# First layer of a four-layer network: order of its recurrent half against its slot routing, and the arithmetic of its slot update

## The chip, the cores and the metric

The kernel is one launch on one core of a Trainium2 chip. The metric is the device time of that launch in microseconds (us). All data is float32. Four batch elements of 1024 tokens with 128 features each go through four layers one after the other; every layer has an "attention" half and a "feed-forward" half, each followed by a residual sum and a layer norm.

## The reference, cut to what matters

Only the first layer is touched by the change. Its attention half is two stacked minGRU layers; its feed-forward half routes every token to 8 of 64 slots, updates the slots by a GRU step, lets the slots attend to one another, and reads them back.

```python
# attention half, twice in sequence (x, then its own result)
z  = sigmoid(x @ Wz.T + bz);  g = max(x @ Wh.T + bh + 0.5, sigmoid(x @ Wh.T + bh))
h_t = (1 - z_t) * h_{t-1} + z_t * g_t           # h_0 = 0.5, over the 1024 tokens
x = layernorm(x + h)

# feed-forward half
h = gelu(concat(x, mean(slots)) @ w1 + b1);  logits = (h @ w2 + b2) / (|tau| + 0.1)
alpha = softmax over the 8 largest logits of a token, 0 for the other slots
si = (alpha^T @ x) / (sum_t alpha + 1e-8)                       # 64 slots x 128
r = sigmoid(si @ Wih_r.T + bih_r + S @ Whh_r.T + bhh_r);  z likewise
n = tanh(si @ Wih_n.T + bih_n + r * (S @ Whh_n.T + bhh_n))
S_new = (1 - z) * n + z * S
q, k, v = S_new @ wq + bq, S_new @ wk + bk, S_new @ wv + bv
y = S_new + softmax(q @ k^T / sqrt(32)) @ v
y = (y - mean) * rsqrt(var + 1e-5) * ln_g + ln_b
slot_values = y @ wvp + bvp
out = (alpha @ slot_values) @ wo + bo
x = layernorm(x + out)
```

(The reference writes the minGRU in logarithms; the recurrence above is the same function.) `S` is the same initial slot table for every batch element.

## The kernel before, in words

The first layer is written as Python generators, one for each batch element or pair of elements. `weave` takes a list of generators and advances each of them to its next `yield` in turn; that gives the program its order. The engines do not run in just that order: a planner reorders the written program, by priority (earlier written first) and by when it believes inputs and buffers to be ready. In the trace, the first slot-update matmul (`pg<-slots`) runs at 78.66 us, ahead of the first routing matmul at 82.70 us, though it is written after it. Once planned, every engine works through its own queue in order.

- `l0_gru(b)` is the attention half of one batch element. It transposes the tokens to features, then does four steps (two layers by two halves of 512 tokens). A step is a matmul `ph` and a sigmoid (line 209), a VectorE combination into `gru_g` (line 211), a matmul `pz` and two sigmoids (217, 219), a GpSimd product (221) and a VectorE scan (223) that writes a half of a tile `gru_h`. Then the result is transposed back, added to `x` (234) and normalised by `norm_parts` (lines 151 to 164), which ends with a transposed copy into `xT` (136). All four batch elements are woven, each with two PSUM banks of its own.
- `l0_slots` prepares what does not depend on the tokens.
- `l0_route(b)` is the routing of one element: gelu (283), logits, the top 8 (293, 294), exp (301), the transposed weights `alT` (315), and the slot input, which ends in `siT` (332), one tile for each pair of elements.
- `l0_update(i)` is the slot update of one pair; it needs `siT` of the pair and ends in `svo` (449).
- `l0_read(b)` needs `svo` and `alT`; it finishes the first layer for one element. `l1_measure(b)` and `l1_choose` begin the second layer.

The stages are: all four `l0_gru`; then `route(0), route(1)`; then `update(0), route(2), route(3)`; then `update(1)` with `read` and `measure` of 0 and 1; then `choose(0)` with `read` and `measure` of 2 and 3. The eight PSUM banks are divided anew at two places: four pools of two during the GRU, and then `u=2, p0=3, p1=3`, where `u` is for the update and `p0`, `p1` are for two batch elements each. A new pool's bank can be written once the last user of that bank in the old pool is done.

Of the kernel before, what the change touches and what calls it, by code (L numbers as in the profile page):

```python
# [10 lines left out]
F32 = mybir.dt.float32  # L11
I32 = mybir.dt.int32
U32 = mybir.dt.uint32
AF = mybir.ActivationFunctionType
ALU = mybir.AluOpType
AX = mybir.AxisListType

B, T, D = 4, 1024, 128
P = 128
# [39 lines left out]
class Net:  # L59
# [124 lines left out]
    def l0_load(self, pool):  # L184
        def ld(name, *shape):
            return self.load(name, list(shape), pool)

        return dict(
            w1=ld("w_slot1", P, 2, DH),
            w2=ld("w_slot2", DH + 1, NS),  # L190
            wg=ld("w_gru", P, 2, 3 * D),
            wa=ld("w_slota", P, 2 * DQ + 3 * D),
            rows=ld("slot_rows", NS, 3, D),
        )

    def l0_gru(self, b, ps, w, nb, wp):

        nc = self.nc
        self.to_features(self.xN[b], b, 0, NC, ps)
        yield  # L200
        src = self.xT[b]
        for ly in range(2):
            hv = wp.tile([P, T], F32, name="gru_h", bufs=8)
            for h in range(2):
                s = slice(h * 512, h * 512 + 512)
                ph = ps([P, 512], "ph")
                self.mm(ph, w[:, 2 * ly + 1, :], src[:, s])
                g = wp.tile([P, 512], F32, name="gru_g")
                nc.scalar.activation(g, ph, AF.Sigmoid, bias=self.col(f"bh{ly}"))

                nc.vector.scalar_tensor_tensor(
                    g, ph, nb[:, 2 + ly : 3 + ly], g, ALU.add, ALU.max
                )
                pz = ps([P, 512], "pz")
                self.mm(pz, w[:, 2 * ly, :], src[:, s])
                z = wp.tile([P, 512], F32, name="gru_z")
                nc.scalar.activation(z, pz, AF.Sigmoid, bias=self.col(f"bz{ly}"))
                a = wp.tile([P, 512], F32, name="gru_a")
                nc.scalar.activation(a, pz, AF.Sigmoid, bias=nb[:, ly : ly + 1], scale=-1.0)
                yield  # L220
                nc.gpsimd.tensor_mul(z, z, g)
                yield
                nc.vector.tensor_tensor_scan(
                    hv[:, s], a, z, hv[:, 511:512] if h else 0.5, ALU.mult, ALU.add
                )
                yield
            src = hv
        r = wp.tile([P, T], F32, name="gru_h", bufs=8).rearrange("p (c d) -> p c d", d=D)
        for h in range(2):
            c1 = 4 * h  # L230
            pt = ps([P, 4, P], "pt")
            for c in range(4):
                self.tr(pt[:, c, :], src[:, (c1 + c) * P : (c1 + c + 1) * P])
            nc.vector.tensor_add(r[:, c1 : c1 + 4, :], pt, self.xN[b][:, c1 : c1 + 4, :])
            yield
            yield from self.norm_parts(wp, r[:, c1 : c1 + 4, :], b, c1, 4, ps=ps, act=True)
            yield


    def l0_slots(self, W, sp):  # L240
# [9 lines left out]
        pb = self.psb("g0", [DH, 1], "pb")  # L250
# [9 lines left out]
        brz = sp.tile([P, 3], F32, name="brz")  # L260
        for i in range(3):
            nc.vector.tensor_add(
                brz[:, i : i + 1], self.col("bih", i=i), self.col("bhh", i=i)
            )
        W.update(s2=s2, hb=hb, rt=rt, brz=brz)
# [4 lines left out]
        W["svo"] = [sp.tile([NS + 1, 2, D], F32, name=f"svo{i}") for i in range(2)]  # L270
        for i in range(2):
            nc.sync.dma_start(out=W["svo"][i][NS : NS + 1], in_=self.io["s_bo2"])
# [62 lines left out]
    def l0_update(self, i, ps, W, wp):  # L335
# [3 lines left out]
        wg, wa, rows, brz = W["wg"], W["wa"], W["rows"], W["brz"]  # L339
        wq, wk = wa[:, 0:DQ], wa[:, DQ : 2 * DQ]  # L340
        wv, wvp, wo = (wa[:, 2 * DQ + j * D : 2 * DQ + (j + 1) * D] for j in range(3))
# [3 lines left out]
        for j in range(2):  # L345
            pg = ps([P, BS], "pg")
            w = slice(j * D, (j + 1) * D)
            self.mm(pg, wg[:, 1, w], s2, start=True, stop=False)
            self.mm(pg, wg[:, 0, w], si, start=False, stop=True)

            g = wp.tile([P, BS], F32, name=f"gate{j}")
            nc.vector.tensor_scalar(g, pg, brz[:, j : j + 1], 0.5, ALU.add, ALU.mult)
            nc.scalar.activation(g, g, AF.Tanh)
            nc.vector.tensor_scalar(g, g, 0.5, 0.5, ALU.mult, ALU.add)
            rz.append(g)
        yield
        pn = ps([P, 2, BS], "pn")
        self.mm(pn[:, 1], wg[:, 1, 2 * D :], s2)
        self.mm(pn[:, 0], wg[:, 0, 2 * D :], si)
        nn = wp.tile([P, BS], F32, name="nn")  # L360
        nc.vector.scalar_tensor_tensor(
            nn, pn[:, 1], self.col("bhh", i=2), rz[0], ALU.add, ALU.mult
        )
        nc.vector.tensor_add(nn, nn, pn[:, 0])
# [5 lines left out]
        nc.vector.tensor_mul(snf, snf, rz[1])  # L370
        nc.vector.tensor_add(snf, snf, nn)
# [3 lines left out]
        for w, nm in ((wq, "s_bq"), (wk, "s_bk")):  # L375
            pq = ps([DQ, BS], "pq")
            self.mm(pq, w, snf)
            t = wp.tile([DQ, N, NS], F32, name=f"t_{nm}")
            nc.vector.tensor_scalar_add(
                t.rearrange("p b s -> p (b s)"), pq, self.col(nm, DQ)  # L380
            )
            qk.append(t)
        v = wp.tile([NS, N, D], F32, name="sv")
        pv = ps([NS, N, D], "pv")
        for b in range(N):
            self.mm(pv[:, b, :], sn[:, b, :], wv)
        nc.vector.tensor_add(v, pv, rows[:, 0:1, :].to_broadcast([NS, N, D]))
        yield
        psc = ps([NS, N, NS], "psc")
        for b in range(N):  # L390
            self.mm(psc[:, b, :], qk[0][:, b, :], qk[1][:, b, :])
        mx = wp.tile([NS, N], F32, name="smx")
        nc.vector.reduce_max(mx, psc, AX.X)
        at = wp.tile([NS, N, NS], F32, name="sat")
        nc.vector.tensor_tensor(
            at, psc, mx[:, :, None].to_broadcast([NS, N, NS]), ALU.subtract
        )
        nc.scalar.activation(at, at, AF.Exp, scale=DQ**-0.5)
        yield
        nc.vector.reduce_sum(mx, at, AX.X)  # L400
        nc.vector.reciprocal(mx, mx)
        nc.vector.tensor_mul(at, at, mx[:, :, None].to_broadcast([NS, N, NS]))
# [7 lines left out]
        for b in range(N):  # L410
            self.mm(py[:, b, :], sn[:, b, :], self.ident, start=True, stop=False)
            self.mm(py[:, b, :], att[:, b, :], v[:, b, :], start=False, stop=True)

        y = wp.tile([NS, N, D], F32, name="sy")
        nc.vector.tensor_copy(y, py)
        st = wp.tile([NS, N, 6], F32, name="sst")
        mv = wp.tile([NS, N, 2], F32, name="smv")
        for b in range(N):
            nc.vector.bn_stats(st[:, b, :], y[:, b, :])
            nc.vector.bn_aggr(mv[:, b, :], st[:, b, :])  # L420
        yield
        sd = wp.tile([NS, N], F32, name="ssd")
        nc.scalar.activation(sd, mv[:, :, 1], AF.Sqrt, bias=self.epsc[0:NS])
        nc.vector.reciprocal(sd, sd)
# [4 lines left out]
        nc.vector.tensor_mul(y, y, rows[:, 1:2, :].to_broadcast([NS, N, D]))  # L429
        nc.vector.tensor_add(y, y, rows[:, 2:3, :].to_broadcast([NS, N, D]))  # L430
        yield
        pyt = ps([P, N, NS], "pyt")
        for b in range(N):
            self.tr(pyt[:, b, :], y[:, b, :])
        yT = wp.tile([P, BS], F32, name="syT")
        nc.vector.tensor_copy(yT, pyt.rearrange("p b s -> p (b s)"))
        yield
        psv = ps([P, BS], "psv")
        self.mm(psv, wvp, yT)
        svT = wp.tile([P, N, NS], F32, name="svT")  # L440
        nc.vector.tensor_scalar_add(
            svT.rearrange("p b s -> p (b s)"), psv, self.col("s_bvp")
        )
        yield

        pso = ps([NS, N, D], "pso")
        for b in range(N):
            self.mm(pso[:, b, :], svT[:, b, :], wo)
# [385 lines left out]
    def front(self, ctx, w0, W, d, dp):  # L834
# [9 lines left out]
        with ExitStack() as right:  # L844
            with ExitStack() as left:
                sp = left.enter_context(tc.tile_pool(name="slot1", bufs=1))
                wp = left.enter_context(tc.tile_pool(name="slot2", bufs=2))
                with self.banks(g0=2, g1=2, g2=2, g3=2), tc.tile_pool(name="gru", bufs=4) as gp:
                    weave(
                        *(self.l0_gru(b, self.bank(f"g{b}"), self.wgru, nb, gp) for b in range(B))  # L850
                    )
                    self.l0_slots(W, sp)
                left.enter_context(self.banks(u=2, p0=3, p1=3))
                pu, pp = self.bank("u"), [self.bank(f"p{b % 2}") for b in range(B)]
# [5 lines left out]
                route = lambda b: self.l0_route(b, pp[b], W, wp)  # L860
# [4 lines left out]
                weave(route(0), route(1))  # L865
# [23 lines left out]
        return ffn(B - 1)  # L889
# [973 lines left out]
    ("s_b1", 1), ("tau", 1), ("bih", 3), ("bhh", 3), ("s_bq", 1), ("s_bk", 1), ("s_bvp", 1),  # L1863
# [34 lines left out]
def layout(i):  # L1898
# [9 lines left out]
    for n in ("z", "h"):  # L1908
# [11 lines left out]
    a["w_slota"] = np.concatenate([s[k] for k in ("wq", "wk", "wv", "wvp", "wo")], axis=1)  # L1920
    a["slot_rows"] = np.broadcast_to(
        np.stack([s["bv"], s["ln_g"], s["ln_b"]])[None], (NS, 3, D)
    )
    a["s_bo2"] = np.broadcast_to(s["bo"], (1, 2, D))
# [133 lines left out]
```

## Time and profile before

| | us |
|---|---|
| three runs | 2602.92, 2603.18, 2606.44; median 2603.18 |
| the profiled execution | 2598.39, its span 2596.6 |
| GRU stage, from the start to the last `xT` | 0 to 83 |
| routing of elements 0 and 1 | 83 to 113 |
| routing of 2 and 3 with the first slot update | 113 to 150 |
| second slot update, reading and measuring of 0 and 1 | 150 to 204 |
| choosing for 0 and 1, reading and measuring of 2 and 3 | 204 to 259 |
| the rest of the program | 259 to 2596.6 |

PE is TensorE's matmul queue and PEld its weight loads; DVE is VectorE, ACT is ScalarE, POOL is GpSimd, SP issues transfers. Busy time over the whole span is 87% for PE, 61% for DVE, 52% for ACT and 29% for POOL. Shares of the whole span say little about the first 259 us, in which PE is busy for 181 us, DVE for 157, ACT for 119 and POOL for 46. The profiled execution lies 4.8 us below the median of the runs.

### The profile page before, as it was taken

Reading aid. Unit: us, or ns where it says so; the run is one execution under the profiler, and the core shown is the slowest. Engines: PE = TensorE matmul, PEld = TensorE weight load, DVE = VectorE, ACT = ScalarE, POOL = GpSimd, SP = SyncE. Lnnn points to the kernel's source line nnn. Section 1 sums busy time; section 2 is a strip of 40 time slices with the busy share of each in tenths; the row PEclk is TensorE's granted clock in tenths of the full one; section 3 lists DMA queues with packets and bytes.
Section 4 is the critical chain, followed back from the end, with each engine's and each line's share of the span. In section 5 each row is a group of like instructions: output and inputs, shape, how many; then the busy total and the mean of one; then the engine's idle time right before and its main releaser. Section 6 shows DMA issues by size and latency. Waiting matters only on the chain. (4 is left out here: it accounts for less than half of the span.)

```text
span 2596.6 us, 34630 instructions
## 1 busy us (share of the span) xinstructions
PE 2261.8 (87%) x12058; PEld 1478.8 (57%) x12058; DVE 1572.3 (61%) x4110; ACT 1347.3 (52%) x2894; POOL 754.9 (29%) x461
## 2 busy tenths in 40 slices
PE   6687889898999999999999777758898989889898
PEld 2454555544777777777776444414555545455566
DVE  6547644333655656656555487988767687777531
ACT  5542433323555565555544767645656555545434
POOL 4002210000000110110112267577445555656500
PEclk8767889899999999999998879868999989899899
DMA  3001100004000000000003233333222222312100
GB/s 94 0 17 26 34 18 17 9 0 163 23 1 1 7 11 1 10 9 1 10 8 90 79 115 102 94 121 115 64 68 73 66 83 59 93 55 90 43 1 9
DMA packets 110288, 122.20 MB, mean 47 GB/s; under 512 B 15462, under 2 KB 72674, under 8 KB 109730
## 3 DMA queue, kind: packets, MB, share of 16 engines
q1 hardware_dynamic: 103586, 106.16, 13.5%
q0 software_dynamic: 5376, 9.62, 1.2%
q10 hardware_dynamic: 1152, 4.19, 0.5%
q8 instruction: 97, 1.59, 0.2%
q14 instruction: 77, 0.63, 0.1%
HBM read 96.78 MB, written 23.16 MB: 46 GB/s over the span
## 5 line engine op out<-in xcount | busy, mean ns | idle before, releaser
L1729 POOL TENSOR_TENSOR hc<-db,cn 128x1024 f32<-128x1024 f32 x128 | 311.6, 2437 | 338.3 <-PE pys L122 234.6
L122 PE MATMUL pys<-hc,sb_c_ident 128*128 128x512 f32 x512 | 278.2, 660 | 38.3 <-POOL hc L1729 38.3
L122 PEld LDWEIGHTS py<-wH,hh 128*128 128x128 f32 x2048 | 252.6, 195 | 97.0 <-ACT hh L1824 49.0
L1119 DVE SCALAR_TENSOR_TENSOR num<-po,sb_c_trig,nsin 128x65 f32<-128x65 f32 x512 | 140.4, 280 | 249.6 <-ACT nsin L1116 249.3
L122 PE MATMUL py<-wH,hh 128*128 128x128 f32 x2048 | 260.0, 280 | 30.4 <-ACT hh L1824 25.9
L1717 ACT ACTIVATE da<-dl,aneg 128x512 f32<-128x512 f32 x256 | 175.4, 690 | 174.0 <-DVE db L1718 171.2
L122 PE MATMUL ph<-xT,wH 128*128 128x512 f32 x512 | 246.6, 607 | 19.8 <-DVE h_acc L1840 11.2
L1116 ACT ACTIVATE nsin<-po,sb_c_trig 128x65 f32<-128x65 f32 x512 | 149.2, 316 | 190.2 <-DVE num L1119 131.8
L1713 POOL TENSOR_TENSOR db<-ud,bn 128x1024 f32<-128x1024 f32 x96 | 236.5, 2467 | 28.4 <-DVE ud L1684 8.8
L1824 ACT ACTIVATE hh<-ph,sb_cols 128x512 f32<-128x512 f32 x256 | 168.7, 681 | 104.0 <-PE ph L122 101.4
L1718 DVE TENSOR_TENSOR_SCAN db<-da,carry,db 128x512 f32<-128x512 f32 x128 | 159.2, 1269 | 78.6 <-POOL db L1713 70.6
L1718 DVE TENSOR_TENSOR_SCAN db<-da,db 128x512 f32<-128x512 f32 x128 | 151.7, 1209 | 47.2 <-POOL db L1713 30.4
L122 PEld LDWEIGHTS pys<-hc,sb_c_ident 128*128 128x128 f32 x512 | 98.9, 211 | 131.6 <-issue 80.8
L122 PE MATMUL pqk<-xT,wE 128*128 128x256 f32 x512 | 168.8, 413 | 2.7 <-ACT r_q L1026 1.7
L994 POOL MEMSET cv<- 128x16 f32 x32 | 4.0, 128 | 570.6 <-ACT cv L1011 448.9
L1083 PE MATMUL po<-cv,a 128*128 128x130 f32 x1024 | 160.4, 283 | 0.4 <-DVE num L1119 0.3
L122 PEld LDWEIGHTS ph<-xT,wH 128*128 128x128 f32 x512 | 91.6, 193 | 118.1 <-issue 76.5
L1083 PEld LDWEIGHTS po<-cv,a 128*128 128x128 f32 x1024 | 137.8, 192 | 14.3 <-issue 1.8
L1326 POOL DMA_INDIRECT xrows<-xN,di x64 | 61.7, 965 | 271.0 <-ACT r_k L1026 120.8
L1840 DVE SCALAR_TENSOR_TENSOR h_acc<-py,gt,h_acc 128x128 f32<-128x128 f32 x256 | 72.2, 341 | 104.5 <-PE py L122 104.5
L122 PE MATMUL ph<-wF,xgT 128*128 x184 | 106.0, 661 | 16.5 <-DVE mh L1410 7.0
L126 PE MATMUL pt<-sb_c_ident,xN 128*128 128x128 f32 x256 | 66.6, 353 | 59.0 <-ACT xN L164 34.6
(407 smaller groups left out, 4568.4 us busy)
## 6 DMA issues: line engine op xcount, KB each, us to landing
bn<-rows SPq DMA_DIRECT2D x128, 256.0 KB, 3.3
cn<-rows SPq DMA_DIRECT2D x128, 256.0 KB, 3.2
xrows<-zero SPq DMA_DIRECT2D x4, 1472.0 KB, 13.8
xg<-xrows SPq DMA_DIRECT2D x20, 256.0 KB, 2.7
yrows<-ys SPq DMA_DIRECT2D x20, 256.0 KB, 2.3
wH<-in_wH ACTq DMA_DIRECT2D x8, 512.0 KB, 5.0
wF<-in_wF SPq DMA_DIRECT2D x1, 3072.0 KB
xN<-in_x SPq DMA_DIRECT2D x8, 256.0 KB, 4.2
```

Source lines behind the costliest of these rows:

```text
L122: self.nc.tensor.matmul(out=out, lhsT=lhsT, rhs=rhs, start=start, stop=stop)
L126: self.nc.tensor.transpose(out, in_, self.ident[0:n, 0:n])
L1083: self.nc.tensor.matmul(out=u["po"][i][:, c, :], lhsT=u["a"][:, i, c, :], rhs=Q["v"][c][:, 2 * hp + i, :, :].rearrange("p a d -> p (a d)") ...
L1116: nc.scalar.activation(t, po[i][:, c, VW : 2 * VW], AF.Copy, scale=trig[:, k, 1:2])
L1119: nc.vector.scalar_tensor_tensor(num[:, c, i, :], po[i][:, c, 0:VW], trig[:, k, 0:1], t, ALU.mult, ALU.add)
L1326: i = nc.gpsimd.indirect_dma_start(out=rows[:, :], out_offset=bass.IndirectOffsetOnAxis(ap=st["dest"][k][:, c : c + 1], axis=0), in_=self. ...
L1713: (nc.vector if n % 4 == 1 else nc.gpsimd).tensor_mul(db, ud, bc[0])
L1717: nc.scalar.activation(da, dl[:, ec, :], AF.Exp, scale=aneg[:, j : j + 1])
L1718: nc.vector.tensor_tensor_scan(db[:, ec, :], da, db[:, ec, :], carry[:, ec, n : n + 1] if h else 0.0, ALU.mult, ALU.add,)
L1729: nc.gpsimd.tensor_mul(hc, db, bc[1])
L1824: nc.scalar.activation(ht, ph, AF.Relu, bias=self.col("h_b1", i=e * NK + k))
L1840: nc.vector.scalar_tensor_tensor(acc[:, c, :], py[:, c, :], gt[:, c, e : e + 1], acc[:, c, :], ALU.mult, ALU.add,)
```

## The change: what it does

First, the order. `l0_gru` of elements 0 and 1 is woven alone. Then `route(0)` and `route(1)` are woven with `l0_gru` of elements 2 and 3, which use the same two pairs of PSUM banks (`g0`, `g1`) that elements 0 and 1 had; the routing gets two banks for each of `p0` and `p1` in this stage, instead of three. The tile `gru_h` has 6 buffers instead of 8. The later stages are woven as before.

Second, the slot update. The sigmoid gates are kept as tanh values (sigmoid(v) = 0.5 + 0.5 tanh(v/2)), with the bias and the factor inside the ScalarE instruction, and the remaining halves and ones go into three-operand VectorE instructions; `S @ Whh_n.T + bhh_n` is computed once. The softmax is left undivided, its sum comes out of the exp instruction, and the division is made when `y` is formed. The bias of `v` is added to `S_new` (each row of the softmax sums to one). The scale `ln_g`, the projection `wvp` and the projection `wo` are multiplied into one matrix `wc` at the start, and `ln_b`, `bvp` and `bo` into one row, which stands in the last row of `svo`. For this, `w_slota` grows by 128 columns and `slot_rows` shrinks to one row.

```diff
 def l0_gru(...):
-            hv = wp.tile([P, T], F32, name="gru_h", bufs=8)
+            hv = wp.tile([P, T], F32, name="gru_h", bufs=6)
...
-        r = wp.tile([P, T], F32, name="gru_h", bufs=8)...
+        r = wp.tile([P, T], F32, name="gru_h", bufs=6)...
 def l0_slots(self, W, sp, ps):
+        brz[:, i] = (bih_i + bhh_i) * 0.5                       # two columns
+        ph = ps([P, 2 * NS], "ph")
+        self.mm(ph, W["wg"][:, 1, 2 * D :], s2.rearrange("p b s -> p (b s)"))
+        nc.vector.tensor_scalar(hn, ph, self.col("bhh", i=2), 0.5, ALU.add, ALU.mult)
+        self.mm(pw, wvpT, wo)
+        nc.vector.tensor_scalar_mul(wc, pw, self.col("ln_g"))
+        self.mm(pc, wvp, self.col("ln_b"))
+        nc.vector.tensor_add(cb[:, NS : NS + 1], pc, self.col("s_bvp"))
+        self.mm(pr, cb, wo)
+        nc.sync.dma_start(out=bo[NS : NS + 1], in_=self.io["s_bo"])
         for i in range(2):
-            nc.sync.dma_start(out=W["svo"][i][NS : NS + 1], in_=self.io["s_bo2"])
+            for b in range(2):
+                nc.vector.tensor_add(W["svo"][i][NS:NS+1, b, :], pr[NS:NS+1], bo[NS:NS+1])
 def l0_update(...):
-            nc.vector.tensor_scalar(g, pg, brz[:, j : j + 1], 0.5, ALU.add, ALU.mult)
-            nc.scalar.activation(g, g, AF.Tanh)
-            nc.vector.tensor_scalar(g, g, 0.5, 0.5, ALU.mult, ALU.add)
+            nc.scalar.activation(g, pg, AF.Tanh, bias=brz[:, j : j + 1], scale=0.5)
...
-        self.mm(pn[:, 1], wg[:, 1, 2 * D :], s2)
...
+            if nm == "s_bq":
+                nc.scalar.activation(tf, pq, AF.Identity, bias=self.col(nm, DQ))
+            else:
+                nc.vector.tensor_scalar_add(tf, pq, self.col(nm, DQ))
...
         nc.vector.reduce_max(mx, psc, AX.X)
-        nc.vector.tensor_tensor(at, psc, mx..., ALU.subtract)
-        nc.scalar.activation(at, at, AF.Exp, scale=DQ**-0.5)
-        nc.vector.reduce_sum(mx, at, AX.X)
-        nc.vector.reciprocal(mx, mx)
-        nc.vector.tensor_mul(at, at, mx...)
+        nc.vector.tensor_scalar_mul(mx, mx, -(DQ**-0.5))
+        for b in range(N):
+            nc.scalar.activation(at[:, b], psc[:, b], AF.Exp, bias=mx[:, b], scale=DQ**-0.5, accum_out=sm[:, b])
+        # pv = sn @ wv, copied by ScalarE; psn = transposed sn, y = psn + bv; sm = 1 / sm
...
         for b in range(N):
-            self.mm(py[:, b, :], sn[:, b, :], self.ident, start=True, stop=False)
-            self.mm(py[:, b, :], att[:, b, :], v[:, b, :], start=False, stop=True)
-        nc.vector.tensor_copy(y, py)
+            self.mm(py[:, b, :], att[:, b, :], v[:, b, :])
+            nc.vector.scalar_tensor_tensor(y[:, b], py[:, b], sm[:, b], y[:, b], ALU.mult, ALU.add)
...
-        nc.vector.tensor_mul(y, y, rows[:, 1:2, :]...)
-        nc.vector.tensor_add(y, y, rows[:, 2:3, :]...)
...
-        self.mm(psv, wvp, yT)
-        nc.vector.tensor_scalar_add(svT..., psv, self.col("s_bvp"))
         for b in range(N):
-            self.mm(pso[:, b, :], svT[:, b, :], wo)
+            self.mm(pso[:, b, :], yT[:, b, :], W["wc"])
 def front(...):
-                with self.banks(g0=2, g1=2, g2=2, g3=2), tc.tile_pool(name="gru", bufs=4) as gp:
-                    weave(*(self.l0_gru(b, self.bank(f"g{b}"), self.wgru, nb, gp) for b in range(B)))
-                    self.l0_slots(W, sp)
+                gru = lambda b: self.l0_gru(b, self.bank(f"g{b % 2}"), self.wgru, nb, gp)
+                with self.banks(g0=2, g1=2, p0=2, p1=2), tc.tile_pool(name="gru", bufs=4) as gp:
+                    weave(gru(0), gru(1))
+                    self.l0_slots(W, sp, pp[0])
+                    weave(route(0), route(1), gru(2), gru(3))
                 left.enter_context(self.banks(u=2, p0=3, p1=3))
...
-                weave(route(0), route(1))
                 weave(update(0), route(2), route(3))
```

## The prediction, made before the changed kernel was run

> **What bounds it now.** I read the table of busy time by stage first, then groups of instructions, waits and the order in time inside those stages. Columns: stretch, length, then busy us and instruction count of each engine, granted TensorE clock, DMA share, GB/s.
>
> ```profile
> 14.00:60.00 46.00, 30.12 (x72) 13.12 (x70) 37.06 (x40) 28.56 (x47) 19.09 (x16) 0.88 0.17 53
> 60.00:83.00 23.00, 13.55 (x55) 8.75 (x56) 14.45 (x89) 18.01 (x48) 0.00 (x0) 0.65 0.00 0
> 83.00:113.00 30.00, 19.70 (x96) 12.63 (x95) 11.72 (x64) 13.30 (x24) 3.93 (x4) 0.72 0.00 1
> 113.00:139.00 26.00, 16.54 (x105) 12.81 (x103) 15.51 (x78) 9.61 (x22) 2.33 (x2) 0.74 0.01 1
> 139.00:150.00 11.00, 5.83 (x23) 3.69 (x24) 4.75 (x17) 2.95 (x4) 0.00 (x0) 0.58 0.00 0
> 150.00:192.00 42.00, 34.96 (x145) 24.80 (x146) 17.25 (x81) 20.72 (x42) 0.00 (x0) 0.62 0.09 25
> 192.00:204.00 12.00, 11.82 (x72) 5.76 (x69) 11.49 (x32) 0.59 (x2) 0.00 (x0) 1.00 0.01 2
> 204.00:259.00 55.00, 39.51 (x170) 25.72 (x168) 42.73 (x119) 16.32 (x36) 14.20 (x12) 0.69 0.13 30
> ```
>
> Only the GRU stretch (14 to 60) has a loaded engine, DVE at 37.06 of 46. From 60 to 150 there is none: PE is at 48 to 66%, DVE at 39 to 63%. These 90 us are dependences in single file, and work put beside them can hide. From 192 to 204 DVE is full.
>
> VectorE in the GRU (start, length), then GpSimd:
>
> ```profile
> 20.82 1.22 DVE L223 TENSOR_TENSOR_SCAN gru_h<-gru_a,gru_z 128x512 f32<-128x512 f32 x1 [1.45 <-POOL gru_z L221]
> 24.14 2.27 DVE L223 TENSOR_TENSOR_SCAN gru_h<-gru_a,gru_z 128x512 f32<-128x512 f32 x1 [0.79 <-POOL gru_z L221]
> ```
>
> ```profile
> 22.83 2.50 POOL L221 TENSOR_TENSOR gru_z<-gru_z,gru_g 128x512 f32<-128x512 f32 x2 [2.04 <-ACT gru_a L219]
> ```
>
> The same scan takes 2.27 instead of 1.22 us when a product is in flight: the two do not overlap. So a step costs scan 1.22 + product 1.27 + part of 0.73 (line 211). Measured pace: the first scan starts at 14.19, the sixteenth ends at 60.30; (46.1 - 1.25) / 15 = 2.99 us.
>
> Waits from 85 to 150 us (total, times, longest):
>
> ```profile
> POOL al L308 <- DVE es L306: 33.0, 3, 24.5
> DVE top L293 <- ACT lg L289: 13.1, 2, 12.0
> PEld pt L126 <- POOL al L308: 11.4, 2, 10.4
> PEld pq L122 <- DVE sn L371: 8.6, 1, 8.6
> ```
>
> Each engine waits for the next in routing; the last line is the update standing behind the top-8 work in VectorE's queue.
>
> **What the Trainium skill says.** "SBUF — State Buffer", section "Who interferes with whom": a VectorE instruction with two SBUF inputs and a GpSimd instruction that reads SBUF exclude each other; the 2.27 us scan agrees. "ScalarE: Activation LUTs", "What ACT_TABLE_LOAD costs": 1.28 us a load and 1.38 us draining, 2.66 in all. The trace agrees on the load (1283 ns, all 12 in the first 262 us) but shows no draining: a tanh ends at 154.84, the load runs 154.86 to 156.14, a sqrt starts at 156.15. I use 1.28. The same page, "Table sets: the hidden batching unit": sigmoid, sqrt, gelu and exp anchor different sets, tanh comes along with some; loads stand at those changes here, and the tanh at 115.06 follows gelu with none. "TensorE: Matmul & The Clock Gate", "What's actually happening": the array is clocked at half rate after idling; the clock here is 0.58 in the emptiest stretch and 1.00 in the fullest.
>
> **Part 1, the order.** The first pair needs 8 steps: 14.2 + 7 x 2.99 + 1.25 = 36.4. Two banks per element don't slow it: one element's ring is matmul 0.86 + sigmoid 0.69 + line 211 0.73 = 2.3 us, and it has two slots of 2.99 to do it in. Six `gru_h` buffers are all held by the first pair, so the second cannot finish a scan much before 33; I count its steps from 36.4.
>
> From there to the point where `xT` of all four and `siT` of 0 and 1 exist (112.6 now):
> - VectorE: 8 steps x 2.99 = 23.9, norms of four (row 60-83) 14.45, routing of two (row 83-113) 11.72; 50.1 in all, to 86.5. Below: steps at their busy time, 37.06 / 16 = 2.32, give 81.
> - ScalarE: half of 28.56 = 14.3, norms 18.0, routing without its three loads and the early gelus of the next pair about 10.5; 42.8, to 79.2, plus 1.28 for each table load.
> - After either, the last normalise, transposes and copy: from 78.48 (last `ln_nm`) to 83.1 now, 4.6 us.
>
> Sigmoids of the second pair now stand in one ScalarE queue with sqrt, gelu and exp. That queue is in order: a gelu that waits for its matmul holds the sigmoids behind it, and through them GpSimd and the scans. How many loads result no row shows. Below: about 6, one per kind and phase. Above: 24 sigmoids and 14 others (8 sqrt, 4 gelu, 2 exp) make at most 28 changes. I take 9, 11.5 us. The stretch ends at 36.4 + 42.8 + 11.5 + 4.6 = **95.3, that is 17.3 earlier**.
>
> Moved past other queues: 8 products on POOL (10.2 us) now share with the two `al` products (2.0) and the one-row memsets; POOL has 45 us free. Routing with two banks instead of three: between 0 and 1.5 us on a logits matmul that waits for a bank; taken as 0, covered by the second pair's steps. The update's first bank waits for the second pair's last transpose: 0, since `route(2)` needs that `xT` as well. SP issues one transfer fewer (241 ns), the weights come to 320 KB as before, and land by 15 us, long before use: 0.
>
> **Part 2, the update.** From 137.67 to 149.44 it runs alone; read from starts in that stretch:
> - gone: subtraction 0.32, sum 0.31, reciprocal 0.19, product 0.34, copy of `y` 0.45, identity passes 0.9, two row operations 0.98, `psv` and its bias 1.24: 4.7;
> - new: scaling the maximum 0.15, a second exp 0.31, two accumulator reads 0.19 each (beside line 315), adding `y` in two pieces instead of a copy about 0.5: 1.3.
>
> Net 3.4 on the path. The gates lose two VectorE operations (0.35 and 0.22), but the chain then stands from 117.62 to 125.35 behind the top 8: 0 there. The scores no longer follow `pv` in the queue, but may still stand behind the 16 `psi` passes (131.9 to 137.7): a gain of 0 to 6, I take 2. The stage becomes 37 - 5.4.
>
> The second update's `svo` is ready at 191.9 and first used at 203.67, so its chain is worth 0. It only frees queues in 150-192: PE about 1.6 us, VectorE 2.5. I take 2 (0 to 5). Next late is the measuring, PE then DVE.
>
> The precomputation is four small matmul groups and a dozen VectorE operations of 0.12 to 0.35 us, in waits before 60: 0 to 1, taken as 0. If those waits are gone it is 1 us on the GRU.
>
> **Sum.** 17.3 + 5.4 + 2 = 24.7. Against the profiled execution (2598.4, span 2596.6 and 1.8 around it) this gives 2573.7. That one lies 4.8 below the median, and I set the forecast from the median: 2603.2 - 24.7 = **2578.5 us**. Everything from 259 on should shift whole; a changed planned order there is worth -8 to +8, 0.3% of 2337.
>
> **The rivals.**
> - *Forecast, overlap works* (0.67): its own range is 2560 to 2594.
> - *More is gained* (0.08): 5 loads leave VectorE the bound (91.1, 21.5 earlier); the scores pass `psi` (9.4), measuring gains 5; 2603.2 - 36 = 2567, with a favourable remainder 2558. For it: 60 to 150 has no full engine.
> - *The second pair isn't hidden* (0.15): the routing is written ahead and shares queues, so the second pair's steps come after it. Then 36.4 + 13 (norms of two) + 30 + 24 + 13 = 116, 3.4 later; with 7.4 from the update, 2599. For it: in-order queues, and the 1.0 us al products. Against: the trace shows work of a later stage planned into earlier gaps.
> - *Table loads become the bound* (0.10), slower: ScalarE needs 42.8 of the 58.9 us; each load adds 1.28. The gain is 36.2 - 1.28n, n counted over both stretches to `svo`: zero at n = 28, and beyond measurement at 33. With 36, alternating in the update too, 2613. At the page's 2.66 it would turn at 14. Against: the trace's price, and only 14 other functions.
>
> A measurement of this kernel can tell about 0.2% (5.2 us) from no change. Faster: forecast 0.66, more 0.08, a third of the third case 0.05, together 0.79; same 0.11; slower 0.10. The range is 2557 to 2603.
>
> **What would show it.** First-pair scans end near 36 and the second's after; `siT` of 0 and 1 and the last `xT` by 95; about 9 more loads there; `svo` of the first pair near 127 instead of 149.4; the first `mall` reduction near 168 instead of 192; the stretch from 204 keeping 55 us. Wrong if the second pair's scans only start after `al`, if ScalarE is above 90% with over 20 loads, or if stretches after 259 differ by over 8 us.

## The result, and the profile after

The changed kernel takes 2608.9 us (median of 14 runs, 2605.6 to 2611.9) against 2604.2 us for the kernel before (14 runs, 2601.0 to 2606.6): the ratio is 1.0019, with a 95% interval of 1.0011 to 1.0027. The forecast was 2578.5 us, in a range of 2557 to 2603. The profiled execution of the changed kernel takes 2607.4 us, its span 2605.6.

In the first layer nothing is gained or lost on the whole. The last `mall` reduction, which ends it, ends at 259.0 us in both kernels. These are the moments inside, in us:

| | before | after | forecast |
|---|---|---|---|
| scans of the first pair end | (woven) | 35.3 | 36.4 |
| first `ph` matmul of the second pair | (woven) | 60.9 | 36.4 |
| ninth scan begins (after: the second pair's first) | 39.0 | 73.0 | |
| last scan ends | 60.3 | 98.1 | |
| last `xT` | 83.1 | 114.4 | 95.3 |
| `siT` of elements 0 and 1 | 112.6 | 83.1 | 95.3 |
| first update matmul that reads `siT` | 114.2 | 114.4 | 95 |
| first `svo` | 149.4 | 149.9 | 127 |
| `siT` of elements 2 and 3 | 138.8 | 144.3 | |
| first `mall` reduction | 192.1 | 193.3 | 168 |

The routing of 0 and 1 and the second half of the GRU have changed places: one is 30 us earlier, the other 31 us later. The next stage needs both, and starts where it did. It then ends later than it could, since the routing of 2 and 3 in it has lost its head start. Before, the `xT` of 2 and 3 was there at 83, and the eight first matmuls of their routing ran from 110.2 to 114.2, in gaps of the routing of 0 and 1. After, only two of the eight run early, at 106.1, and the other six from 115.8 to 120.8. The last `psi` passes (the products that give the slot input) then come 5.2 us later, first before and then after:

```profile
135.78 1.96 PE L122 MATMUL psi<-xN,al 128*64 128x128 f32 x16
```

```profile
140.97 1.96 PE L122 MATMUL psi<-xN,al 128*64 128x128 f32 x16
```

The table of busy time by stage of the kernel after, in the same stretches as before (stretch, length, then busy us and instructions of PE, PEld, DVE, ACT and POOL, the granted clock, DMA share, GB/s):

```profile
14.00:60.00 46.00, 29.80 (x112) 17.14 (x111) 26.16 (x75) 30.75 (x56) 10.22 (x8) 0.81 0.17 56
60.00:83.00 23.00, 18.16 (x77) 10.41 (x77) 18.97 (x71) 17.84 (x30) 7.18 (x7) 0.85 0.00 0
83.00:113.00 30.00, 15.62 (x49) 7.52 (x48) 17.77 (x54) 20.96 (x40) 6.29 (x5) 0.76 0.00 1
113.00:139.00 26.00, 16.91 (x78) 11.42 (x78) 13.49 (x69) 12.98 (x25) 2.04 (x2) 0.63 0.00 1
139.00:150.00 11.00, 7.96 (x54) 6.32 (x53) 4.40 (x17) 4.82 (x10) 0.00 (x0) 0.81 0.00 1
150.00:192.00 42.00, 34.59 (x134) 25.96 (x134) 14.61 (x72) 20.71 (x46) 0.00 (x0) 0.55 0.09 25
192.00:204.00 12.00, 12.00 (x69) 5.65 (x68) 10.70 (x31) 1.15 (x2) 0.00 (x0) 1.00 0.00 1
204.00:259.00 55.00, 39.34 (x178) 26.07 (x175) 43.50 (x122) 16.92 (x37) 14.19 (x12) 0.69 0.14 31
```

The forecast expected stretches to fill up. They did not: VectorE, at 37.06 of 46 us before, is down to 26.16 in the GRU stretch, and ScalarE, which was to be the bound, has 17.84 of 23 and 20.96 of 30 us. In none of these stretches from 14 to 150 is an engine full (82% at most). What each waits for between 34 and 75 us (total, times, longest):

```profile
POOL hT L303 <- PE pl L122: 26.3, 2, 25.5
DVE top L318 <- ACT lg L314: 11.4, 1, 11.4
PEld pt L126 <- ACT xN L164: 6.8, 5, 5.7
POOL gru_z L221 <- ACT gru_z L217: 6.8, 1, 6.8
```

GpSimd, which multiplies for every GRU step, does nothing for 25.5 us, and the first thing that it then does is a memset of the routing. VectorE stands 11.4 us ahead of the top-8 work. PE, in order of time (start, length):

```profile
50.52 3.47 PE L126 MATMUL pt<-sb_c_ident,xN 128*128 128x128 f32 x14 [4.79 <-ACT xN L164]
...
56.35 1.20 PE L126 MATMUL pt<-sb_c_ident,xN 128*128 128x128 f32 x9
57.39 3.68 PE L122 MATMUL pl<-sb_w_slot,hT 65*128 65x64 f32 x32
60.91 1.81 PE L122 MATMUL ph<-xT,sb_wA 128*128 128x512 f32 x2
```

PE stood idle for 4.79 us while the second pair's tokens were long in place (with banks of their own, below, their transposes are copied from 30.7 on). Here their first transposes are among those at 50.52 and 56.35, mixed with the last of the first pair's norms, which hold the same banks `g0` and `g1`; then come the routing's logits (57.39), and only then the second pair's first step (60.91). Then ScalarE:

```profile
62.80 1.28 ACT L209 ACT_TABLE_LOAD   x1 [1.11 <-PE ph L122]
64.10 0.69 ACT L209 ACTIVATE gru_g<-ph,sb_cols 128x512 f32<-128x512 f32 x1
64.80 1.28 ACT L326 ACT_TABLE_LOAD   x1
66.10 0.72 ACT L326 ACTIVATE ex<-ex,rt 128x512 f32<-128x512 f32 x1
66.84 1.28 ACT L217 ACT_TABLE_LOAD   x1
```

A sigmoid of the GRU, an exp of the routing and the next sigmoid stand alternately in its queue, with a load ahead of each. There are 11 loads between 36 and 113 us.

The update is late for further reasons. PE in the kernel after, then VectorE, around the first update's scores:

```profile
124.45 0.62 PE L122 MATMUL pq<-sn,sb_w_slota 128*32 128x128 f32 x4
134.05 0.66 PE L122 MATMUL psc<-t_s_bk,t_s_bq 32*64 32x64 f32 x4 [8.98 <-DVE t_s_bk L402]
134.81 1.92 PE L126 MATMUL pt<-sb_c_ident,al 128*64 128x128 f32 x8
136.66 3.39 PE L122 MATMUL psi<-xN,al 128*64 128x128 f32 x16
...
142.77 0.60 PE L122 MATMUL pv<-sb_w_slota,sn 128*64 128x128 f32 x4
```

```profile
133.37 0.32 DVE L331 RECIPROCAL es<-es 128x8 f32<-128x8 f32 x2
133.61 0.28 DVE L402 TENSOR_SCALAR t_s_bk<-pq,sb_cols 32x128 f32<-32x128 f32 x1
```

`pq` is ready at 125, and its 0.28 us bias is added at 133.61, behind all of VectorE's routing work for elements 2 and 3. `pv`, which needs only `sn` (ready at 121.5), then stands behind 32 `psi` passes. What the new update saves ahead of these two waits is lost in them. What it saves behind them counts: from the first matmul after the `psi` passes to the end of `svo` it now takes 7.1 us (142.8 to 149.9), and 11.8 before (137.7 to 149.4).

So the theory to test was: **the second pair is held by banks that go round in the order of writing, and then by queues whose order is fixed**; table loads are the rival that the prediction itself had named. The update should be worth something by itself, and more if it is planned ahead of the routing.

### The profile page after: what moved, and what is told of

Same layout as the page of the kernel before. It is cut to its first block, busy times and chain, and to the rows that moved or that the text cites. A ratio compares the mean times of both kernels' runs of the same rounds, so it can differ in the third digit from the quotient of the medians.

```text
span 2605.6 us, 34628 instructions
## 1 busy us (share of the span) xinstructions
PE 2264.9 (87%) x12054; PEld 1484.3 (57%) x12054; DVE 1574.3 (60%) x4099; ACT 1363.9 (52%) x2914; POOL 754.2 (29%) x461
## 5 line engine op out<-in xcount | busy, mean ns | idle before, releaser
L122 PE MATMUL pys<-hc,sb_c_ident 128*128 128x512 f32 x512 | 272.7, 649 | 36.5 <-POOL hc L1749 36.5
L122 PE MATMUL ph<-xT,wH 128*128 128x512 f32 x512 | 248.9, 612 | 20.4 <-DVE h_acc L1860 12.1
L1346 POOL DMA_INDIRECT xrows<-xN,di x64 | 61.8, 965 | 270.7 <-ACT r_k L1046 120.8
```

What stands on the lines that cost most here:

```text
L122: self.nc.tensor.matmul(out=out, lhsT=lhsT, rhs=rhs, start=start, stop=stop)
L1346: i = nc.gpsimd.indirect_dma_start(out=rows[:, :], out_offset=bass.IndirectOffsetOnAxis(ap=st["dest"][k][:, c : c + 1], axis=0), in_=self. ...
```

## The experiments

In all tables "first layer" is the end of the last `mall` reduction in the profiled execution. The kernels ran on several chips; each ratio is to the kernel before on the same chip, and its median there is given where it differs from 2604 us. On the chips where that median is 2640 to 2647 us, the end of the first layer comes late by itself. It is a loop of 64 matmuls (`pm`), which takes 11.3 us in the kernels before and after and in the first four experiments, and 13.3 to 17.0 us in all others, with PE idle in between and, in the two of 17.0, with a granted clock of 0.50 for 5 us; the changed kernel itself takes 11.3 on one chip and 13.3 on another, and so ends its first layer at 259.0 and at 261.5. Why PE stands idle there was not found. The first matmul of the choosing (`px`) comes ahead of this loop and is the better mark between chips: the changed kernel has it at 228.3 on the one and 228.7 on the other, and the kernel before at 227.1. In the expectations, A is the theory of the banks, C that of ScalarE's queue with its table loads; the later ones split C into L (the loads) and Q (the fixed order).

### Each half of the change by itself

The new update in the old order:

```diff
 the change, but
-    weave(gru(0), gru(1)); ... weave(route(0), route(1), gru(2), gru(3))   # shared banks, 6 gru_h
+    weave(gru(0), gru(1), gru(2), gru(3)); ... weave(route(0), route(1))   # as before, 8 gru_h
```

> The new slot update with the old order of stages (all four recurrent halves first). Theory A (the second pair is held back by the two pairs of PSUM banks that it shares with the first; the shorter update only waits longer behind the psi passes in TensorE's queue): first svo written between 147 and 150 us as before (149.0), total within 3 us of before. Rival B (the update's shortening is real and the new order loses it): svo at 144 to 146, total 4 to 7 us below before.

Ratio 0.9983 (0.9977 to 0.9990), 2599.3 us. First `svo` at 145.4 instead of 149.4, first layer 254.4 instead of 259.0. The arithmetic gains 4.6 us, as rival B said.

The new order with the old update:

```diff
 the kernel before, but front() as in the change, and gru_h with 6 buffers
```

> The new order of stages with the old slot update. Theory A: second pair's first scan at about 73 us and last transposed copy near 114 us as in the changed kernel, first svo at 148 to 152, total 0 to 6 us above before. Rival B: the order itself costs 6 us or more, total 2609 or more.

Ratio 1.0009 (1.0003 to 1.0016), 2606.7 us. First `svo` at 155.2, later than the 148 to 152 of theory A, and first layer 265.5: 6.5 us later, of which the whole time shows only 2. The next stage starts where it did (its first matmul on `siT` at 114.8), and its last `psi` passes come 6.1 us later (141.9 against 135.8): the lost head start of the routing of 2 and 3. With the new update the order costs 4.6 us (254.4 to 259.0), and in the new order the new update gains 6.5 (265.5 to 259.0). The two halves cancel; neither was without effect.

### What holds the second pair

Banks of their own, order of writing as in the change:

```diff
-    with self.banks(g0=2, g1=2, p0=2, p1=2), ...
+    with self.banks(g0=2, g1=2, g2=2, g3=2), ...      # gru(b) and the first route(b) use g{b}
```

> The changed kernel with two PSUM banks for each of the four recurrent halves (as before the change); the routing of elements 0 and 1 takes over the banks of the recurrent halves of 0 and 1, so the update's banks are free once routing 0 is done. Theory A: the second pair's matmuls start before 35 us instead of 60.9, its last transposed copy ends by 95 (114.4 in the changed kernel), first svo by 135, total 2580 to 2592. Rival C (it is held back by its place in the program, behind the routing, and by table loads in ScalarE's queue): last transposed copy still after 108, total within 4 us of the changed kernel.

The second pair's first matmul moves from 60.9 to 33.7, its first scan from 73.0 to 41.0. That much was the banks. But the last scan still ends at 96.5 and the last `xT` comes at 113.4: eight steps now take 55.5 us instead of 25.1. Freed at the start, it loses the time on the way, and rival C's signs, a last `xT` after 108 and a total within 4 us of the changed kernel's, are the ones that came. (First layer 254.9; ratio 1.0003, 0.9994 to 1.0011.)

The second pair written ahead of the routing, banks as in the change:

```diff
-    weave(route(0), route(1), gru(2), gru(3))
+    weave(gru(2), gru(3), route(0), route(1))
```

> The changed kernel with gru(2), gru(3) ahead of route(0), route(1) in the weave; banks shared as in the changed kernel. Theory A: the banks still hold it back: second pair's first matmul not before 55 us, total within 4 us of the changed kernel (2605 to 2613). Rival C (place in the program): it starts near 40 us and the total falls by 10 us or more.

First matmul at 59.5, last `xT` at 117.1, first layer 258.9, ratio 1.0009 (1.0000 to 1.0017). Priority over the routing is worth nothing while the first pair's norms are written ahead in the same banks.

Are the table loads the second brake? (They are the loads that stand in ScalarE's queue wherever it changes between functions like these.) The changed kernel and the one with own banks, each with one table set for the whole stretch: the square root of the GRU's norms, the gelu and the exp of the routing are computed as sigmoid instead. The values are other ones, and each of the two was timed once, so only the moments of one execution are read.

```diff
-    AF.Sqrt (norms of the GRU), AF.Gelu, AF.Exp (l0_route)
+    AF.Sigmoid
```

> The changed kernel with the square root of the GRU's norms, the gelu and the exp of the routing all computed as sigmoid (so their values are other ones), the planned order otherwise nearly kept: no table load is left between 36 us and the update. Theory L (table loads set the pace once the second pair has its banks): the first step of the second pair stays at about 59 to 61, since the banks still hold it, but with 11 loads of 1.28 us gone the last xT comes at 99 to 104 instead of 114.4. Rival Q (ScalarE's fixed order and single file set the pace, loads or not): the last xT stays at 109 or later. Rival A (banks alone): start and end both within 2 us of the changed kernel's.

Not one load is left between 7.3 and 132 us, and the last `xT` comes at 114.1 instead of 114.4, where theory L had 99 to 104. ScalarE at the same place as above:

```profile
59.71 0.69 ACT L209 ACTIVATE gru_g<-ph,sb_cols 128x512 f32<-128x512 f32 x1 [0.39 <-PE ph L122]
60.51 0.69 ACT L217 ACTIVATE gru_z<-pz,sb_cols 128x512 f32<-128x512 f32 x1
61.09 0.68 ACT L219 ACTIVATE gru_a<-pz,nbz 128x512 f32<-128x512 f32 x1
61.66 0.72 ACT L326 ACTIVATE ex<-ex,rt 128x512 f32<-128x512 f32 x1
```

All three sigmoids of the first step are done by 61.8, eleven microseconds earlier than in the kernel after, and yet its scan starts at 71.03 instead of 72.96. VectorE shows why:

```profile
65.29 1.40 DVE L211 SCALAR_TENSOR_TENSOR gru_g<-ph,nbz,gru_g 128x512 f32<-128x512 f32 x2
66.61 3.08 DVE L328 TENSOR_TENSOR ex<-ex,rep 128x512 f32<-128x512 f32 x2
69.61 1.26 DVE L330 TENSOR_REDUCE es<-ex 128x8 f32<-128x512 f32 x2
70.79 0.31 DVE L331 RECIPROCAL es<-es 128x8 f32<-128x8 f32 x2
71.03 3.09 DVE L223 TENSOR_TENSOR_SCAN gru_h<-gru_a,gru_z 128x512 f32<-128x512 f32 x2
```

The step's own VectorE instruction (65.29) comes after both elements' top-8 work, and its scan after the routing's products and sums. The loads had been hidden in a wait for VectorE's queue. They are not free in the next stage: one of the two last `xT` copies came at 110.5 instead of 113.8, the update had its bank with it, and its first matmul on `siT` ran at 111.2 instead of 114.4, the first `svo` at 146.0 instead of 149.9. All loads together are worth 3 to 4 us there, not the 10 to 15 of theory L.

> The kernel with banks of their own for all four elements, and the same three functions computed as sigmoid. The second pair starts at about 34. Theory L: its 13 or 14 loads gone (17 us), the last xT comes at 95 to 99 instead of 113.4. Rival Q: sigmoids still stand in ScalarE's queue behind gelus, exps and normalisations that wait for others; the last xT stays at 106 or later. A mixture gives 100 to 105.

With own banks the loads count for more: with 14 of them fewer up to the last `xT`, 18 us of ScalarE, that comes at 108.6 instead of 113.4, and the last scan ends at 90.7 instead of 96.5. (First `svo` 138.6 instead of 146.0; the routing of 2 and 3 has fewer loads too.) Most of the delay stays. PE in this kernel:

```profile
74.57 1.91 PE L126 MATMUL pt<-sb_c_ident,al 128*64 128x128 f32 x8 [4.66 <-POOL al L333]
76.41 3.18 PE L122 MATMUL psi<-xN,al 128*64 128x128 f32 x16
79.53 1.06 PE L126 MATMUL pt<-sb_c_ident,al 128*64 128x128 f32 x8
82.24 0.25 PE L126 MATMUL pt<-sb_c_ident,si 64*128 64x64 f32 x1 [1.65 <-DVE rd L351]
82.41 1.12 PE L122 MATMUL pz<-gru_h,sb_wA 128*128 128x512 f32 x2
```

The `pz` matmul of a GRU step (82.41) waits in PE's queue behind four groups of the routing's, of which two wait in their turn for GpSimd and VectorE. The second pair runs at the pace of the routing's single file, because it was planned into its gaps. This is Q, with PE and VectorE in it beside ScalarE.

If the order is the cause, another order must help. The steps can be written in three groups, so that no GRU step is mixed with the routing: first pair's scans; second pair's scans with the first pair's norms; second pair's norms with the first pair's routing.

```diff
 own banks, 8 gru_h, and
-    weave(gru(0), gru(1)); l0_slots; weave(route(0), route(1), gru(2), gru(3))
+    g = [gru(b) for b in range(B)];  scans = lambda b: islice(g[b], 13)
+    weave(scans(0), scans(1)); l0_slots
+    weave(scans(2), scans(3), g[0], g[1])
+    weave(route(0), route(1), g[2], g[3])
```

> The new update with own banks and eight gru_h buffers, written in three groups: first pair's scans; second pair's scans beside the first pair's norms; second pair's norms beside the first pair's routing. In the planned ScalarE queue all sigmoids but none stand behind a gelu or an exp, and the sets change only about 8 times up to siT. Theory Q (and L): last scan at 61 to 66, siT of 0 and 1 at 93 to 99, last xT at 95 to 105, first svo at 128 to 138, last mall at 238 to 249, the whole 6 to 16 us below before. Rival (the overlap itself costs as much as it brings, by VectorE and GpSimd excluding each other): last scan after 75, last mall at 253 or later.

Ratio 0.9964 (0.9951 to 0.9977; before 2643.7 here). Last scan at 76.4 instead of 96.5, last `xT` at 109.0, `siT` of 0 and 1 at 99.3, first `svo` at 140.9, first layer 252.6. The direction is Q's, the size is half of what was expected: the last scan was to end at 61 to 66, and `svo`, `xT` and the first layer miss their ranges too. The rival's first sign showed (a last scan after 75), its second just not. Its reason, VectorE and GpSimd excluding each other, isn't what the trace shows. Twelve us of what is missing lie between two scans, at 53.2 and 65.0. ScalarE there:

```profile
60.27 0.69 ACT L217 ACTIVATE gru_z<-pz,sb_cols 128x512 f32<-128x512 f32 x1
63.72 0.59 ACT L136 COPY xT<-pt 128x512 f32<-128x512 f32 x1 [2.75 <-PE pt L126]
64.20 0.69 ACT L219 ACTIVATE gru_a<-pz,nbz 128x512 f32<-128x512 f32 x1
```

The sigmoid `a` of a step stands behind the copy of `xT`, which waits for the transposes of the first pair's norms; the scan that needs it waited 8.10 us. The norms' chain is shorter than the routing's, but work that is mixed with it still goes at its pace.

The same grouping with the old update:

> The old update with the grouped order (own banks, eight gru_h buffers): the new order's idea by itself. If order and update are worth about the same apart as together: siT of 0 and 1 at 97 to 101, last xT at 107 to 111, first svo at 143 to 147 (149.4 before), last mall at 254 to 258 (259.0 before), ratio 0.997 to 0.9995. Rival (the grouped order's gain was all the update's): last mall at 259 or later, ratio 1.0 or above.

Ratio 0.9972 (0.9961 to 0.9983; before 2639.6 here), first `svo` 143.2, last `xT` 105.5, first layer 255.8. The order by itself, with banks of its own, is worth 3 to 4 us when it is written so (3.2 at the end of the first layer, 4.0 at the first `px`), where the change's order costs 6.5. The rival, that all was the update's gain, is excluded.

And the grouping with the banks shared as in the change, so that only the order of writing differs from it (and `gru_h` has 8 buffers):

> The changed kernel with its own two pairs of banks, g0 and g1 shared by the elements, but written in the three groups (and eight gru_h buffers): only the order of writing differs from the changed kernel. Theory W (a bank goes round in the order of writing, and the changed kernel wrote the first pair's norms ahead of the second pair's steps): the first step of the second pair comes at 33 to 37 instead of 61 with the same banks, the last scan at 74 to 84, the last xT at 106 to 113, last mall at 251 to 257. Rival B (two banks for two elements are too few): the first step at 50 or later, or the last xT still at 114 and last mall at 258 or later.

The second pair starts at 36.9: with the same banks, another order of writing frees its start, as banks of its own do. But the end is a miss, as in rival B's second sign: last scan at 83.4, last `xT` at 116.6, first layer 262.4 (of which 5.7 is the longer loop). For what follows the start, two banks for two elements are too few: an element's second step waits for the first pair's transposes in the same bank (its next `ph` came at 49.9), and those wait for the norms. Its ratio is 0.9978 (0.9966 to 0.9991; before 2647.2), although its profiled first layer is no shorter (`px` at 229.2); see the remainder below.

Start and end of the second pair, by what was freed:

| | order of writing as in the change | in groups |
|---|---|---|
| shared banks | starts 60.9, last scan 98.1, `px` 228.3, first layer 259.0 | 36.9, 83.4, 229.2, 262.4 |
| own banks | 33.7, 96.5, 223.1, 254.9 | 33.4, 76.4, 219.4, 252.6 |

The left column has six `gru_h` buffers and the right one eight. The buffers are not what held the second pair: with own banks and six of them, the scans of its first layer begin at 41.0 and those of its second at 83.0, in buffers that were last read by matmuls at 28.9 and transposes at 45.3.

### The update behind the routing

The new update in the old order, with the four `yield`s up to its exps taken out, so that it has priority over the top-8 work of elements 2 and 3:

```diff
 the new update by itself, and in l0_update, as far as the exps,
-        yield          # four times
```

> The order of the kernel before with the new update, and the update planned ahead of the routing of 2 and 3 up to its exps. If standing behind top-8 and psi is what kept the new update's gain small: first svo at 134 to 141 instead of 145.4 with the new update alone, last mall at 247 to 253 instead of 254.4, ratio to before 0.995 to 0.998. Rival: the routing of 2 and 3 then ends later by as much and the time stays at 0.998 to 1.0.

Ratio 0.9956 (0.9941 to 0.9972; before 2639.6). First `svo` at 135.9 instead of 145.4, first layer 250.5. VectorE with the new update alone, and then with it ahead:

```profile
125.59 0.68 DVE L325 TENSOR_TENSOR rep<-rep,pl 128x512 f32<-128x512 f32 x1
126.19 0.28 DVE L388 TENSOR_TENSOR sn<-slots,nn 128x128 f32<-128x128 f32 x1
```

```profile
118.59 0.28 DVE L386 TENSOR_TENSOR sn<-slots,nn 128x128 f32<-128x128 f32 x1
118.98 0.28 DVE L387 SCALAR_TENSOR_TENSOR sn<-gate,sn 128x128 f32<-128x128 f32 x1
119.32 0.28 DVE L388 SCALAR_TENSOR_TENSOR sn<-sn,nn 128x128 f32<-128x128 f32 x1
```

In the first, `sn` comes after both elements' top-8 work, though its input was ready at 118.9 (PE waited 8.6 us for `sn`); in the second it goes between. `siT` of 2 and 3 comes 3.7 us later (143.4 against 139.7); the second update waits for that, but it has time: its `svo` comes at 163.8, and the reading of 2 and 3 is a stage later.

The same in the grouped kernel with own banks:

> As the grouped kernel, and the four points at which the update up to its exps lets the routing of 2 and 3 go ahead are removed, so its VectorE operations are planned ahead of the top-8 work. If the update's wait behind top-8 and psi is on the path: first svo 4 to 10 earlier than in the grouped kernel and last mall 2 to 8 earlier. If the routing of 2 and 3 then ends last: siT of 2 and 3 later by 2 to 6 and last mall within 2 us.

Ratio 0.9929 (0.9900 to 0.9957; before 2643.7; seven runs, 2617 to 2636). First `svo` at 131.1, first layer 247.8: 11.2 us less than before, and 13.4 less at the first `px`. Of all versions this one has the shortest first layer.

### The remainder after the first layer

Both kernels end the first layer at 259.0, and from there every engine has the same instructions in the same order, and still the medians differ by 4.7 us.

> The changed kernel as it is, beside the others. Its first layer ended with that of before (last mall 259.3 and 259.0), while its median lay 4.7 us above. If that remainder belongs to the kernel, the ratio is again 1.001 to 1.003 here; if it came from that set of executions, the ratio is within 0.9985 to 1.001.

Ratio 0.9994 (0.9980 to 1.0008; before 2639.6): the 0.2% is not found again. (The 259.3 in this expectation is 259.0 in the trace.) Where time goes in the later stages can be seen by comparing this execution with the first one of the same program, 33.7 us shorter. The two run level to about 250 us; 2 us come in the loop of `pm` matmuls, 9 us at 270 to 310, around the transfers that gather the chosen rows, and 15 us near 1400, in one transfer pattern. The issue of the same transfer on SP, first execution and then this one:

```profile
1395.95 0.36 SPq L1399 DMA_DIRECT2D xg<-xrows  x1
1402.49 0.36 SPq L1399 DMA_DIRECT2D xg<-xrows  x1
```

```profile
1409.23 0.36 SPq L1399 DMA_DIRECT2D xg<-xrows  x1
1426.86 0.36 SPq L1399 DMA_DIRECT2D xg<-xrows  x1
```

Two issues that were 6.5 us apart are 17.6 us apart. So the time after 259 us holds hand-offs by transfer that differ from one execution to another with nothing changed. Which of them made the 4.7 us, and why it held over 14 runs on that chip, stays open; and so does the part of the other ratios that the first layer doesn't explain (for the grouped kernel with the update ahead 7 to 8 of 19 us, for the grouped one with shared banks all of it). With own banks the 4.1 us won in the first layer don't show in the time at all, and of the 6.5 us lost by the new order with the old update only 2 do. The verdicts above therefore rest on the moments in the first layer.

## Why the prediction was wrong

- **First pair done at 36.4**: right (35.3), with two banks for each element.
- **"I count its steps from 36.4": this step failed.** The second pair's first matmul came at 60.9 and its first scan at 73.0. The prediction checked the `gru_h` buffers for this start and not the banks: its own text has the same two pairs of banks going to the second pair, whose transposes and first `ph` then stand behind the first pair's norms, written ahead in them. That is 24.5 us (own banks, or another order of writing, start it at 33 to 37). The pace was right once it ran: 25.1 us for eight steps, forecast 23.9.
- **"The stretch ends at 36.4 + 42.8 + 11.5 + 4.6 = 95.3": failed as a method.** It is a sum of ScalarE's busy times, which holds only if ScalarE's queue is always full. ScalarE was busy for 17.84 of 23 and 20.96 of 30 us. The prediction had seen the danger ("that queue is in order: a gelu that waits for its matmul holds the sigmoids behind it") and gave it no number. In the changed kernel it shows as the 12.1 us from the second pair's first matmul to its first scan; with own banks it is the larger part, and the eight steps took 55.5 us.
- **Table loads**: 9 forecast, 11 came. The 11.5 us charged for them were too much: without any of them the last `xT` moved by 0.3 us, the first `svo` by 3.9. The tail rival (loads as the bound) is excluded for this kernel; with own banks 14 loads cost 4.8 us at the last `xT`, 0.34 for each.
- **"The update's first bank waits for the second pair's last transpose: 0"**: `siT` was ready at 83.1 and the update started at 113.8. `route(2)` does need the same transpose, as the reason said, but the update needs only `siT`, and stood 31 us for a bank. (With own banks its first matmul on `siT` ran at 94.3; `svo` then still came at 146.0, behind the routing of 2 and 3.)
- **The routing of 2 and 3: put at nothing.** Part 1 takes "the early gelus of the next pair" out of the stretch and charges them nowhere. Before, they and their matmuls had run in gaps of the stage ahead; with the second pair's `xT` at 114 most of them can't. The last `psi` passes come 5.2 us later (6.1 with the old update), and `svo`, which needs TensorE after them, waits for that.
- **The update, 5.4 + 2: nearly right in size.** By itself it brought 4.0 at `svo` (149.4 to 145.4) and 4.6 at the end of the layer; in the new order 5.3 (155.2 to 149.9) and 6.5. The 2 us for the scores were no gain: the scores did go ahead of the `psi` passes (130.5 with the new update alone), but `pv`, which now follows them, stood behind (138.3). Planned ahead of the routing, the update is worth 8.5 (259.0 to 250.5).
- **The rest after 259**: no more than -8 to +8 was allowed; the profiled executions differ by 9.0 there, the medians by 4.7.
- **Readings of the table**: from 60 to 150 PE is at 53 to 66%, not 48, and ScalarE was left out, which is at 78% from 60 to 83: that stretch had less room than "none" says. In the second case 2567 less 8 is 2559, not 2558.

The nearest of the cases is the third, to which the prediction gave 0.15: "the routing is written ahead and shares queues, so the second pair's steps come after it", with the next stage at 116 (it was 114.4). That this is so near is in part luck. Written ahead of the routing, the second pair started at 59.5 all the same: its start was held by the first pair's norms in the shared banks, which no case names. Its price, 2599, is 9.9 us below the result. In the first layer the order cost 6.5 us where it had 3.4, and the update brought 6.5 where it had 7.4; 4.7 came after 259 us, and the median of the kernel before is 1.0 higher over 14 runs than over the first three. Of the signs of being wrong, two showed: the second pair's first scan started at 72.96, after the first `al` at 70.2, and the stretches after 259 differ by 9.0 us. The third did not: ScalarE is at 70 to 78% from 60 to 113, with 11 loads. The forecast of the likeliest case had the evidence of idle engines for it; idle time says that there is room, not that the order of the queues lets the work in.

## What to carry to other kernels

Before putting two chains beside each other, list for each queue and each ring of buffers what stands ahead of the moved work, in the order in which it is written: here a ring (buffers or banks that are handed out in turn) served its users in that order, and mixed queues went at the pace of the slowest chain in them. Then give that a time; the sum of an engine's busy times is only the least that the stretch can take. Ask also which later stage loses a head start. Work that the next stage waits for (here the slot update) is worth moving ahead of bulk work that is needed a stage later: that brought about as much as rewriting its arithmetic (3.9 and 4.6 us).

## What the runs showed of the hardware that was not expected

- Table loads in strict alternation cost 1.28 us each and nothing beside it: a sigmoid and an exp alternate at 2.0 us each (64.10, 66.10 and 68.13), which is a load and the 0.7 us instruction. Where ScalarE's results wait in VectorE's queue anyway, taking all of them out moved the last `xT` by 0.3 us and the first `svo` by 3.9.
- One and the same program took 2605.6 us in one profiled execution and 2639.3 in another, on another chip, with the mean granted clock at 0.920 and 0.912; at 240 us the two were 0.4 us apart. Most of the rest came at a few transfers, not evenly.
- In these two executions one and the same loop of 64 matmuls took 11.3 and 13.3 us, with PE idle in between in the second.
